# Mamba stages: every queue in the source's order, stores a slot later, less on VectorE, X for one pair

## The chip, the cores and the metric

The kernel runs on one core of one Trainium2 chip, in one launch, in float32. The metric is the device time of the execution in microseconds. A core has five instruction queues that matter here: TensorE (PE, matmuls), VectorE (DVE), ScalarE (ACT), GpSimd (POOL) and SyncE (SP), which issues the transfers (DMAs).

## The reference, cut to what matters

Four layers follow each other on an image batch of 4 x 96 x 64 x 64: a Mamba layer (0), a state-space layer with four scan directions (1), a second Mamba layer like the first (2), and a ConvNeXt block (3). The change is in the code of layers 0 and 2:

```python
def _mamba_block(seq, ...):                      # twice per layer, each time seq = seq + _mamba_block(seq)
    h = layernorm(seq) * ln_g + ln_b
    xs, z = split(h @ in_w)
    xc = silu(causal_conv4(xs) + conv_b)
    dt, Bm, Cm = split(xc @ xproj_w)
    delta = softplus(dt @ dt_w + dt_b)           # (L, 192)
    dA  = exp(delta[..., None] * A)              # (L, 192, 16)
    dBx = delta[..., None] * Bm[:, None] * xc[..., None]
    h_t = dA_t * h_{t-1} + dBx_t                 # the scan along L = 4096
    y = sum_s(h * Cm) + Dp * xc
    return (y * silu(z)) @ out_w
# afterwards
gp  = relu(x.mean((2, 3)) @ gp_w.T + gp_b)       # pooled from the layer's input
out = fus_w @ concat([mamba_out, gp]) + fus_b
out = batchnorm(out) + residual                  # statistics over batch and space
```

## The kernel before

`mamba_fusion` is one Mamba layer. The four images are taken as two pairs; `X` holds the sequence of all four in SBUF. A **step** is one (pair, block, chunk of 512 positions): 2 x 2 x 8 = 32 steps a layer. The 2 x 192 channels of a pair lie on three tiles `j` of 128 partitions.

A step has two halves that run beside each other:

- `mamba_front` is a generator that makes what the next step will scan: layernorm into `h` (matmul with `center`, square, matmul with `mean`, rsqrt on ACT, multiply on DVE L184, scale on POOL L185), convolution and input projection (`pu`, `pz`), the small projection `pd` and `dbl`, then for each `j` the softplus `delta` and `du = delta * xz`. Softplus is: absolute value, exp, log on ACT; on DVE L267, which adds the log to max(x, 0) from PSUM tile `pt`; an identity L268 on ACT that rounds 1+u and writes it back to the PSUM tile; on DVE L270, which makes the rounding error from that tile and `u`; an addition on POOL L271. `delta` and `du` are stored to DRAM (L251, as `dd` and `dg`), since the scan needs each row spread over 16 partitions.
- `Scan.run` scans the step in 24 **groups**: 3 tiles x 4 quarters `q` x 2 halves, of two blocks of 128 x 512 each. A turn of its loop is a **slot**: slot `n` scans group `n`, and does the other stages for groups ahead and behind.

The stages of a group before, with the slot in which each is issued relative to the scan:

| stage | slot | engine and work |
| --- | --- | --- |
| `load` | 4 ahead | SP: `dd` (and for every fourth group `dg`) spread from DRAM into `da` / `du`, L295; six buffers |
| `decay` | 2 ahead | ACT: two exponentials `da`, L107 |
| `spread` | 1 ahead | PE: two matmuls into PSUM `bs` (two banks' pairs), L313; or, for every fourth group, ACT exponentials into `bs` and POOL `du * B`, L308 |
| `scan` | 0 | DVE: `bs * B` L335 (not for the fourth groups), two scans L340; POOL: `hc = hs * C` L342; ACT: last column to `carry` L345 |
| `sums` | 2 after | PE: two matmuls `py` L361, and for each `j` one with `w_dd` L355 |
| `close`, `project`, `fuse` | 3, 4, 5 after the last group of a tile | DVE: `py * silu(z)` L369; PE: `po` L377; DVE: residual add into X L381; for the second block PE `pf` L510, ACT bias L511, DVE batch statistics L512, SP store L513 |

`run` pulls one piece of the generator per slot, by the tuple `PACE`. The order in which each engine gets its instructions is then set by the framework's scheduler, which reorders independent instructions by its own estimate of costs; every engine works through its own list in order.

## Time and profile before

| what | us |
| --- | --- |
| runs | 9810.94, 9851.49, 9849.05 (median 9849.05) |
| profiled execution | 9796.82 (span 9795.1) |
| first Mamba layer, first scan to last | 78 to 3047 |
| second Mamba layer, first scan to last | 6246 to 9197 |
| busy over the span | PE 8426.9, DVE 8142.4, POOL 6879.1, ACT 5527.9 |

The span is the time from the first to the last instruction of the profiled execution. A group line gives the source line, engine, operation, `out<-in` tiles and shape, the count, then the busy time and the mean of one, then the idle time of that engine just before these instructions and what ended it. A wait line gives who waited for whom, the total, how often, and the longest. PEclk in a table of windows is the share of full clock that TensorE was granted.

### The profile page before, as it was taken

How to read it: one execution, taken by the hardware profiler on the slowest of the kernel's cores; microseconds unless marked ns; L12 is line 12 of the kernel's file. 1: busy time of each engine (PE TensorE's matmuls, PEld its weight loads, DVE VectorE, ACT ScalarE, POOL GpSimd, SP SyncE). 2: the span in 40 equal slices, each digit the busy share in tenths (PEclk: the TensorE clock that was granted, in tenths of full speed). 3: DMA queues.
4: the chain of work that ended last, by engine and by line, in shares of the span. 5: the costliest groups of instructions: out<-in, count | busy, mean ns of one | idle time of the engine just before them, and what ended most of it. 6: DMA issues, size and time to landing. Idle time of an engine off the chain costs nothing. (4 is left out here: it accounts for less than half of the span.)

```text
span 9795.1 us, 110014 instructions
## 1 busy us (share of the span) xinstructions
PE 8426.9 (86%) x32750; PEld 3475.8 (35%) x32750; DVE 8142.4 (83%) x11036; ACT 5527.9 (56%) x10516; POOL 6879.1 (70%) x4573
## 2 busy tenths in 40 slices
PE   7888889888887988998888889788888888888678
PEld 1222212222212776776766767212212222222122
DVE  7999999999995666666666667699999999999887
ACT  5666666665663555555555555466666665666345
POOL 6888888888884555555555555588888888888511
PEclk8999999999997999999999999799999999999789
DMA  6677776777774222222222222576777776776653
GB/s 184 201 205 201 205 207 201 203 202 205 206 208 130 73 67 82 83 66 83 82 73 73 86 68 60 157 204 201 207 206 205 211 203 198 210 205 201 166 119 84
DMA packets 808930, 1525.65 MB, mean 156 GB/s; under 512 B 126190, under 2 KB 131722, under 8 KB 804491
## 3 DMA queue, kind: packets, MB, share of 16 engines
q1 hardware_dynamic: 805258, 1513.50, 54.4%
q8 instruction: 260, 4.26, 0.2%
q10 hardware_dynamic: 3072, 5.11, 0.1%
q14 instruction: 340, 2.78, 0.1%
HBM read 1222.99 MB, written 148.50 MB: 140 GB/s over the span
## 5 line engine op out<-in xcount | busy, mean ns | idle before, releaser
L342 POOL TENSOR_TENSOR hc<-hs,bc 128x1024 f32<-128x1024 f32 x1536 | 3610.9, 2358 | 625.5 <-DVE hs L340 545.8
L340 DVE TENSOR_TENSOR_SCAN hs<-da,carry,bs 128x512 f32<-128x512 f32 x2016 | 2466.5, 1264 | 81.0 <-DVE bs L335 2.8
L107 ACT ACTIVATE da<-da,w_a 128x512 f32<-128x512 f32 x2304 | 1616.9, 716 | 1251.7 <-DMA da<-dd 1191.7
L361 PE MATMUL py<-hc,selsum 128*32 128x512 f32 x6144 | 1797.8, 639 | 445.9 <-POOL hc L342 438.9
L313 PE MATMUL bs<-du,seldu 64*128 64x512 f32 x4608 | 1565.3, 675 | 216.0 <-DVE hs L340 203.7
L335 DVE TENSOR_TENSOR bs<-bs,bc 128x1024 f32<-128x1024 f32 x1152 | 1397.7, 1213 | 166.6 <-PE bs L313 163.1
L308 POOL TENSOR_TENSOR du<-du,bc 128x1024 f32<-128x1024 f32 x384 | 905.3, 2358 | 260.3 <-DMA du<-dg 141.0
L361 PEld LDWEIGHTS py<-hc,selsum 128*32 128x32 f32 x6144 | 239.8, 110 | 1791.8 <-POOL hc L342 1097.0
L917 DVE TENSOR_SCALAR seg<-dr,dac 128x128 f32<-128x128 f32 x1536 | 641.2, 451 | 281.9 <-PE y L962 279.5
L313 PEld LDWEIGHTS bs<-du,seldu 64*128 64x128 f32 x4608 | 444.0, 195 | 1205.2 <-DVE hs L340 864.4
L933 POOL TENSOR_TENSOR seg<-seg,cb 128x384 f32<-128x384 f32 x512 | 515.7, 1009 | 475.5 <-DVE cb L932 409.3
L194 PE MATMUL pu<-h,w_conv 96*128 96x512 f32 (+3 forms) x2048 | 833.4, 627 | 8.5 <-ACT rs L107 8.4
L340 DVE TENSOR_TENSOR_SCAN hs<-bs,carry,du 128x512 f32<-128x512 f32 x672 | 823.6, 1260 | 6.2 <-issue 3.2
L868 PE MATMUL front<-pk,sconv 128*128 128x512 f32 x1536 | 755.2, 609 | 27.7 <-ACT z L856 23.8
L972 POOL TENSOR_TENSOR y<-y,xs 128x192 f32<-128x192 f32 x496 | 295.3, 595 | 603.8 <-DVE y L971 587.9
L985 ACT ACTIVATE y<-yz 128x192 f32<-128x192 f32 x512 | 186.1, 363 | 906.2 <-DVE yz L984 905.5
L937 POOL TENSOR_TENSOR xs<-pre,coef 128x576 f32<-128x576 f32 x512 | 598.9, 1175 | 54.0 <-ACT pre L112 24.8
L879 PE MATMUL front<-sconv,pk 128*128 128x192 f32 x3072 | 572.0, 330 | 55.8 <-DVE pre L884 50.5
L345 ACT COPY carry<-hs 128x2 f32<-128x2 f32 x1344 | 250.9, 187 | 566.1 <-DVE hs L340 562.3
L879 PEld LDWEIGHTS front<-sconv,pk 128*128 128x128 f32 x3072 | 496.7, 190 | 87.7 <-DVE pre L884 76.8
L107 ACT ACTIVATE bs<-da,w_a 128x512 f32<-128x512 f32 x768 | 522.0, 680 | 3.1 <-DVE hs L340 1.6
L962 PEld LDWEIGHTS y<-xs,seg 128*128 128x128 f32 x3072 | 437.7, 204 | 142.0 <-issue 80.7
(209 smaller groups left out, 13623.5 us busy)
## 6 DMA issues: line engine op xcount, KB each, us to landing
da<-dd SPq DMA_DIRECT2D x3072, 256.0 KB
du<-dg SPq DMA_DIRECT2D x768, 256.0 KB
dr<-rows SPq DMA_DIRECT2D x256, 384.0 KB
bc<-rows SPq DMA_DIRECT2D x256, 256.0 KB
dd<-delta SPq DMA_DIRECT2D x192, 256.0 KB
dg<-du SPq DMA_DIRECT2D x192, 256.0 KB
pk<-xn SPq DMA_DIRECT2D x128, 384.0 KB
pk<-xn SPq DMA_DIRECT2D x128, 256.0 KB
```

The lines of the kernel that those rows point to most:

```text
L107: self.last = self.scalar.activation(out, in_, func, **kw)
L194: nc.tensor.matmul(pu[r0:r1], lhsT=wt["conv"][:kk, tap, d0:d1], rhs=h[:kk, b, ds(tap, T)], start=(tap == 0), stop=(tap == 3),)
L308: nc.gpsimd.tensor_tensor(g["du"], g["du"], self.b_or_c(g, 0), ALU.mult)
L313: nc.tensor.matmul(g["bs"][:, i], lhsT=self.sel["du"][rows, g["half"], g["q"]], rhs=g["made"]["du"][rows, g["j"]], start=True, stop=True,)
L335: nc.vector.tensor_tensor(dbx, dbx, self.b_or_c(g, 0), ALU.mult)
L340: nc.vector.tensor_tensor_scan(hs[:, i], da[:, i], dbx[:, i], init, ALU.mult, ALU.add)
L342: nc.gpsimd.tensor_tensor(g["hc"], hs, self.b_or_c(g, 1), ALU.mult)
L361: nc.tensor.matmul(py[rows], lhsT=self.sel["sum"][:, g["q"]], rhs=g["hc"][:, i], start=(g["q"] == 0), stop=(g["q"] == NQU - 1),)
L868: nc.tensor.matmul(p, lhsT=self.conv[:, i, DI + q * DST : DI + (q + 1) * DST], rhs=pk[:, i, ds(c * T, T)], start=(i == 0), stop=(i == 2),)
L879: nc.tensor.matmul(p, lhsT=pk[:, i, ds(c * Q, Q)], rhs=self.conv[:, i, :DI], start=(i == 0), stop=(i == 2),)
L917: nc.vector.tensor_scalar(seg[:, h], g["pair"]["dr"][:, c % 2 * NH + h], made["dac"][:, n0 + h : n0 + h + 1], 0.0, ALU.subtract, ALU.min,)
L937: nc.gpsimd.tensor_tensor(xs, x.to_broadcast([P, 3, NH, HD]), coef.to_broadcast([P, 3, NH, HD]), ALU.mult)
```

## The change

1. **Order.** At the end of each turn of `run`, every instruction that the turn issued is chained to the one before it on its engine, SP included, by a dependency that needs no semaphore. Each engine and the transfer queue so get their instructions in the order in which the source issues them.
2. **Lags.** `load` goes from 4 to 5 slots ahead and its buffers from six to eight; `hc` and `carry` move into `after`, issued in the next slot ahead of that slot's scan; `du * B` moves into `product`, two slots ahead; `sums` go from 2 to 3 slots after, `close` from 3 to 4. `hs` and `hc` have four buffers for three. The generator's layernorm is a four-step pipeline with each consumer a piece later, `pd` and `dbl` have pieces of their own, the softplus is split (`softplus` on ACT, `softplus_rest` on DVE a piece later, POOL another piece later), and every store is issued a piece after what it stores. `PACE` and `LEAD` are set anew.
3. **Softplus tile.** 1+u is written to a tile `w` in SBUF instead of back to the PSUM tile.
4. **VectorE.** The residual add becomes a third matmul into `po` with the identity (first block) or the fusion weight (second block) on X; for the second block `w_out` is multiplied by the fusion weight once per layer, so that the fusion needs no matmul of its own. ACT writes the result to X, for the second block with the sum of each row as a second output; a slot later ACT makes the squares' sum around the chunk's mean, in place of DVE's statistics, and a few tiny instructions at the end of the layer join them.
5. **X for one pair.** `X` holds two images. The second pair's chunk is loaded over the first pair's once that has been stored. The pooled sums of the second pair come from eight loads into the `da` buffers.

The core of the diff:

```diff
+IN_ORDER = mybir.DependencyInfo(mybir.DependencyClass.NoSync, mybir.DependencyReason.DATA)
...
-PACE = (1,) * 8 + (2,) + (1,) * 7 + (2,) + (1,) * 7
-LEAD = 4
+PACE = (1,) * 5 + (2, 1, 1, 1) * 2 + (2,) + (1,) * 10
+LEAD = 5
...
-    nc.vector.scalar_tensor_tensor(out, x, 0.0, t, ALU.max, ALU.add)
-    nc.scalar.activation(x, u, AF.Identity, bias=1.0)
-    nc.vector.scalar_tensor_tensor(t, x, 1.0, u, ALU.subtract, ALU.subtract, reverse1=True)
-    nc.gpsimd.tensor_tensor(out, out, t, ALU.add)
+    w = work.tile([P, T], F32, name="wa", bufs=2)
+    nc.scalar.activation(w, u, AF.Identity, bias=1.0)
+    return work.tile([P, T], F32, name="delta", bufs=2), t, u, w, x
+
+def softplus_rest(nc, out, t, u, w, x):
+    nc.vector.scalar_tensor_tensor(out, x, 0.0, t, ALU.max, ALU.add)
+    nc.vector.scalar_tensor_tensor(t, w, 1.0, u, ALU.subtract, ALU.subtract, reverse1=True)
...
+    for n in range(6):
+        for stored in stores:
+            nc.sync.dma_start(*stored)
+        stores = []
+        if 2 <= n < 5:
+            j = n - 2
+            delta, lost = kept.pop(0)[:2]
+            nc.gpsimd.tensor_tensor(delta, delta, lost, ALU.add)
+            nc.gpsimd.tensor_tensor(du[:, j], delta, xz[:, j], ALU.mult)
+            for name, x in (("dd", delta), ("dg", du[:, j])):
+                made[name, j] = dram.tile([P, T], F32, name=f"{name}{j}")
+                stores.append((made[name, j], x))
+        if 1 <= n < 4:
+            softplus_rest(nc, *kept[-1])
...
-        po = self.psum.tile([P, T], F32, tag="po", name="po", bufs=1)[:C]
+        po = self.po = self.psum.tile([P, T], F32, tag="po", name="po", bufs=1)[:C]
+        xs = self.X[:, b, ds(g["c"] * T, T)]
+        nc.tensor.matmul(po, lhsT=wt["of_x"], rhs=xs, start=True, stop=False)
         for n, (j, r0, r1) in enumerate(ROWS[b]):
             nc.tensor.matmul(
-                po, lhsT=wt["out"][r0:r1, j], rhs=xz[r0:r1, j], start=(n == 0), stop=(n == 1)
-            )
-        xs = self.X[:, 2 * g["pair"] + b, ds(g["c"] * T, T)]
-        nc.vector.tensor_tensor(xs, xs, po, ALU.add)
+                po, lhsT=wt["out"][r0:r1, j], rhs=xz[r0:r1, j], start=False, stop=(n == 1)
+            )
+
+    def keep(self, g, b):
+        xs = self.X[:, b, ds(g["c"] * T, T)]
+        if g["sub"] == 0:
+            self.tc.nc.scalar.copy(xs, self.po)
+        else:
+            self.fuse(g, b, xs, self.po)
...
-            if (g := at(3)) and g["last"]:
+            if (g := at(4)) and g["last"]:
                 self.close(g)
             for stage, lag in (
-                (self.load, -4), (self.spread, -1), (self.decay, -2), (self.scan, 0), (self.sums, 2),
+                (self.load, -5), (self.spread, -1), (self.decay, -2), (self.after, 1),
+                (self.product, -2), (self.scan, 0), (self.sums, 3),
             ):
...
-            for lag, what in ((4, self.project), (5, self.fuse)):
+            for lag, what in (
+                (4, self.project), (5, self.keep), (6, self.spread_out), (7, self.reload)
+            ):
...
+            for ins in traced[start:]:
+                if ins.engine not in self.engines:
+                    continue
+                if ins.engine in last:
+                    self.tc.add_manual_dep(ins, last[ins.engine].name, IN_ORDER, reason="order")
+                last[ins.engine] = ins
...
-        nc.vector.bn_stats(stats[:, b * NT + c], xs)
-        nc.sync.dma_start(dst[b, :, ds(c * T, T)], xs)
+    def fuse(g, b, xs, po):
+        n = (2 * g["pair"] + b) * NT + g["c"]
+        nc.scalar.activation(
+            xs, po, AF.Identity, bias=gb[:, n // NT : n // NT + 1], accum_out=sums[:, n : n + 1]
+        )
+
+    def spread_out(g, b):
+        n = (2 * g["pair"] + b) * NT + g["c"]
+        xs = X[:, b, ds(g["c"] * T, T)]
+        nc.scalar.mul(means[:, n : n + 1], sums[:, n : n + 1], -1.0 / T)
+        sq = work.tile([P, T], F32, tag="ua", name="sqs", bufs=2)[:C]
+        nc.scalar.activation(
+            sq, xs, AF.Square, bias=means[:, n : n + 1], accum_out=squares[:, n : n + 1]
+        )
+        nc.sync.dma_start(dst[n // NT, :, ds(g["c"] * T, T)], xs)
```

In the changed kernel L297 and L299 are the two instructions of `softplus_rest`, L369 is the multiply `bs * B`, L374 the scans, L178 the layernorm's multiply and L408 the multiply of `close`.

## The prediction

> **What bounds the kernel now.** I read the page first (busy shares, the 40 slices), then the table of windows, then the groups by line and the waits inside one steady stretch, then single instructions. "DVE" is VectorE, "PE" TensorE, "ACT" ScalarE, "POOL" GpSimd, "SP" the transfer queue. A step is one chunk of one layer for one pair: 24 groups. A slot is one turn of `run`'s loop.
>
> The page's slices show that the edited code runs twice:
>
> ```profile
> DVE  7999999999995666666666667699999999999887
> ```
>
> The stretches at 9 are the two Mamba stages; by the first and last scan they last from 78 to 3047 us and from 6246 to 9197 us, about 5,920 of 9,795 us. The stage between and the tail are not edited. The windows view gives, for 2,400 us inside the first stage and for two slices of it:
>
> ```profile
> core 0: us, PE busy (x) PEld busy (x) DVE busy (x) ACT busy (x) POOL busy (x), PEclk, DMA share, GB/s
> 400.00:2800.00 2400.00, 2098.09 (x6438) 488.05 (x6438) 2246.40 (x2081) 1496.79 (x2677) 2055.26 (x987) 0.96 0.71 204
> 1800.00:1900.00 100.00, 88.74 (x266) 20.59 (x264) 91.15 (x83) 61.24 (x114) 82.82 (x40) 0.91 0.70 201
> 2700.00:2800.00 100.00, 85.49 (x276) 20.10 (x275) 95.37 (x89) 63.04 (x116) 85.92 (x42) 1.00 0.69 204
> ```
>
> DVE is busy 93.6%, with PE (87%) and POOL (86%) close behind. So DVE sets the pace, and what it can gain by waiting less is 6.4%. The two slices show that DVE loses more when the granted clock is 0.91 than at 1.00. The groups of DVE in that stretch (count | busy, mean ns | idle before, releaser):
>
> ```profile
> L340 DVE TENSOR_TENSOR_SCAN hs<-da,carry,bs 128x512 f32<-128x512 f32 x828 | 1013.0, 1264 | 32.9 <-ACT da L107 0.5 <-ACT carry L345 0.5 <-POOL du L308 0.5
> L335 DVE TENSOR_TENSOR bs<-bs,bc 128x1024 f32<-128x1024 f32 x468 | 567.9, 1214 | 69.9 <-PE bs L313 68.2
> L270 DVE SCALAR_TENSOR_TENSOR lg<-pt,ua 128x512 f32<-128x512 f32 x78 | 53.0, 680 | 16.4 <-ACT pt L268 15.9
> L184 DVE TENSOR_TENSOR h<-pc,rs 96x512 f32<-96x512 f32 x52 | 35.1, 676 | 12.5 <-ACT rs L107 12.3
> L381 DVE TENSOR_TENSOR X<-X,po 96x512 f32<-96x512 f32 x52 | 34.7, 668 | 10.9 <-PE bs L313 10.9
> L512 DVE BATCH_NORM_STATS2 stats<-X 96x6 f32<-96x512 f32 x26 | 17.5, 672 | 0.0
> ```
>
> 468 multiplies at 18 a step are 26 steps: 92.3 us a step. Idle per step: 2.69 us before the multiply (PE late), 0.63 before L270, 0.48 before L184, 0.42 before L381, 0.12 before L267 (its row has 3.1), and about 1.5 in the four scan rows, mostly 0.1 us between the multiply and the scan that reads it. Sum 5.9. Most of the 2.69 falls at one place, where the timeline has 2.08 us of `pd` matmuls ahead of `bs` and DVE idle for 1.77 us at 1530.44. Behind it stand these waits of the other engines:
>
> ```profile
> PE py L361 <- POOL hc L342: 167.0, 209, 4.6
> ACT da L107 <- DMA da<-dd: 463.4, 296, 6.3
> SPq L251 <- POOL delta L271: 197.9, 78, 4.6
> ```
>
> PE stops at `py` for POOL with the next `bs` behind it; loads come late for ACT, partly because SP stands at a store. ACT (62%) has room, so its 463 us cost DVE next to nothing.
>
> **What the Trainium skill says.** *PSUM — Partial Sum Buffer*, "Engine vs sequencer instructions": the queues of ScalarE, VectorE and GpSimd are strict FIFO and matmuls complete in program order; so a wait at a queue's head holds all behind it. The waits above agree. *TensorE: Matmul & The Clock Gate*, "The HAM clock gate": TensorE runs at full or half clock. Here the same pair of `py` matmuls took 1.05 us, or 1.92 us at 1555.84. *SBUF — State Buffer*, "Who interferes with whom": a DVE instruction with two SBUF inputs contends with a GpSimd instruction that reads SBUF, and whichever comes second is blocked until the first has ended. Of the DVE instructions before, none in the steady Mamba steps has two SBUF inputs, but in the stage between L984 has, and L971 reads PSUM:
>
> ```profile
> L984 DVE TENSOR_TENSOR yz<-y,z x512: 336/1020/2630, 3158.0 to 6153.5; 128x192 f32<-128x192 f32 x171
> L971 DVE TENSOR_TENSOR y<-y,edac x496: 336/357/363, 3161.4 to 6152.1; 128x192 f32<-128x192 f32 x166
> ```
>
> The timeline of one case (start us, us):
>
> ```profile
> 3335.43 1.32 DVE L984 TENSOR_TENSOR yz<-y,z 128x192 f32<-128x192 f32 x1
> 3335.39 1.15 POOL L937 TENSOR_TENSOR xs<-pre,coef 128x576 f32<-128x576 f32 x1
> ```
>
> Same work (min/median/max ns), but L984 has a median of 1020: it started 0.04 us after a POOL instruction and ended 0.21 us after that one ended. The trace agrees.
>
> **The change, part by part.**
>
> *Work off DVE.* The residual add (L381) becomes a matmul into the same PSUM bank, the batch statistics (L512) sums that ACT gives with its activations. Both Mamba layers together: 128 adds at 0.668 and 64 statistics at 0.672 us, less the 0.04 us by which neighbours overlap (the rows' counts times means give 2,330 us, the union 2,246, over 2,081 instructions): 192 x 0.63 = **-121 us**, all on DVE's path. ACT takes in exchange two copies a step (0.575 us each) in the first block, two pairs of a tiny multiply (0.19) and a square (0.59) in the second, 1.2 to 1.6 us: 57.6 becomes 59 us of 90, covered. PE gets six projection matmuls for five on average, about +1 us a step: covered by its 13% idle. The shorter X frees memory; its eight loads and reductions for the pooled sum stand in place of two long reductions (4.42 us each) before the first scan; two reloads in 8 steps of a layer wait on SP for their store, with the loads three slots ahead.
>
> *Waits.* Sums move from two to three groups behind the scan, stores go a slot behind, `pd` and `dbl` get slots of their own, loads go five ahead with eight buffers instead of four with six. `h` and the softplus tail come a slot after ACT's part. So L184's 0.48 and L381's 0.42 go, L270's 0.63 falls to 0.2, and of L335's 2.69 the bunched part goes. What is late next is PE at half clock: 0.96 means half speed for 8% of the time, 7.4 us a step, 3.7 us of work lost, and the two `bs` banks give only a slot of slack; projections of 3 x 1.06 us ahead of `bs` add to it. I keep 1.4. Sum -2.6 us a step, x 64: **-166 us** (bounds 0 and -270, all but the turn-around).
>
> *The fixed order.* It issues nothing new. What queues behind each waiting instruction: behind SP's stores the loads, with three slots (11 us) until ACT wants them; behind ACT's softplus the exponentials, two slots early; behind PE's `py` the next `bs`. POOL at the softplus slots has two `hc`, a product (2.36 us each) and twice 1.27 us; I walked it and find it under two slots late, which the sums' third slot covers. Cost taken as nothing; the cover failing is the slow case below.
>
> *A lock that comes in.* L270's successor, L299 of the changed kernel, reads `w` and `u`, both now in SBUF; before, `x` stood in PSUM (the identity L268 wrote it there). Three a step. POOL is busy 86%, mostly with instructions of 2.36 us that read SBUF. Undisturbed the price is small: L1262 of the last stage, the same operation from SBUF, has a median of 752 ns against 680. Against a running POOL instruction it is the rest of that one plus about 0.55. Walk: after the scan of group 14 both L297 (0.68, reads PSUM) and POOL's `hc` start; L299 comes 0.6 us later, waits some 1.75 and takes 2.3: +1.6. The second and third meet the product and the 1.27 us instructions somewhere: +0.35 each. I take +2.3 a step, x 64: **+147 us**. Bounds: +0.07 each, 14 us (no gain: L1262 shows none), and +2.2 each, 420 us.
>
> *Ends.* In each Mamba layer's last step DVE waited 5.01 and 2.55 us for `py` (timeline from 2957): -15 for both. The first exponentials now queue behind the next step's layernorm (about 5 us a layer): +10. The closing statistics are a few tiny instructions, within 2 us.
>
> Sum: -121 - 166 + 147 - 5 = **-145 us**. The profiled execution took 9,796.8 us (span 9,795.1), so it would take about 9,652. The runs shown have a median of 9,849, 0.5% above it; the same difference from there is 9,704, rounded to **9,705**.
>
> **Rivals.** (1) *The lock is cheap*, because L299 mostly gets there first: -121 - 250 + 30 = -341, about 9,510 to 9,560. For: an L984 that met no POOL instruction took 336. Against: POOL's 86%. (2) *No change*: L299 meets the full rest of long instructions (+3.4 a step, 218) and PE gives back only 100 us of waits: -121 - 100 + 218 + 10 = +7, 9,856. (3) *Slower, through PE's fixed order*: at both projections three matmuls stand ahead of `bs`, and in half-clock windows everything takes double. From the point where PE is more than one slot (3.7 us) behind the scan, each us is DVE's. Place: groups 3 and 19 of a step. Price: `bs` waits up by 4 us a step instead of down by 1.3: -121 - 98 (the other waits) + 256 + 147 = +184, 10,030. For: PE at 87%, and 1.77 us lost at one bunch before. Against: in the two slots around each projection a group that needs no `bs` follows, and PE's stops for POOL vanish. (4) *The order is not kept*: excluded, the instruction lists of the changed kernel show it.
>
> **How the numbers follow.** Main case 0.56 (9,705, itself 9,610 to 9,800); cheap lock 0.17; no change 0.13; slower 0.14. About 0.5% (49 us) is what a measurement of this kernel can tell from no change. Faster by more: the main case but 0.02, the cheap lock, a little of the third: 0.73; within: 0.13; slower: 0.14. The range, 9,540 to 9,880, takes in the first three but the edge of the cheap lock.
>
> **What would show it.** Right: no DVE add or statistics in the step; L299 at a mean near 1.4 us with a wide spread; the multiply's wait for PE (L369 there) near 1.4 us a step; ACT's wait for `da` far below 463 us; a step near 90 us. Wrong: L299 near 0.75 (then faster), the multiply's wait above 2.7 us a step (then slower), or DVE waiting for ACT at L297.

## The result, and the profile after

The changed kernel takes 9999.26 us (median of 4 runs, 9986.54 to 10019.13) where the kernel before takes 9845.95 in the same comparison (9810.94 to 9851.49). The ratio is 1.0165 [1.0135, 1.0195]: slower, and outside the predicted range of 9,540 to 9,880. The profiled execution has a span of 9989.0 us against 9795.1, at a mean granted clock of 0.912 against 0.941.

By the first and last scan, the Mamba stages now last from 91.5 to 3134.6 us and from 6348.5 to 9391.1 us, 3043 us each, against 2969 and 2951 before. That is 166 of the 194 us by which the span of the profiled execution grew; the other 28 lie ahead of the first scan of the two layers (13 and 14). So the loss lies in the edited stages. The busy shares of DVE over the 40 slices of the page, and the windows view of 2,400 us inside the first stage:

```profile
DVE  7999999999996666766766667699899999899887
```

```profile
core 0: us, PE busy (x) PEld busy (x) DVE busy (x) ACT busy (x) POOL busy (x), PEclk, DMA share, GB/s
400.00:2800.00 2400.00, 2064.67 (x6272) 473.75 (x6270) 2188.55 (x1935) 1435.76 (x2679) 2015.22 (x954) 0.91 0.75 198
```

DVE's busy time in the stretch fell from 2246 to 2189 us, but the stretch also holds fewer steps, as the groups below show. Per step DVE is busy for 2188.55 / 25.06 = 87.3 us, before 2246.40 / 26 = 86.4: the work taken off DVE doesn't show in its busy time, since the three L299 of a step are longer (1.4 us together) and the instructions overlap their neighbours less (1.2 us). The larger part of the loss is waiting, and the groups say for what (count | busy, mean ns | idle before, releaser):

```profile
L374 DVE TENSOR_TENSOR_SCAN hs<-da,carry,bs 128x512 f32<-128x512 f32 x796 | 975.3, 1267 | 46.8 <-DVE bs L369 1.4
L369 DVE TENSOR_TENSOR bs<-bs,bc 128x1024 f32<-128x1024 f32 x451 | 547.1, 1213 | 28.5 <-PE bs L343 28.5
L299 DVE SCALAR_TENSOR_TENSOR lg<-wa,ua 128x512 f32<-128x512 f32 x75 | 85.8, 1145 | 8.5 <-ACT wa L291 0.5 <-ACT da L111 0.5
L408 DVE TENSOR_TENSOR xz<-py,xz 128x512 f32<-128x512 f32 x75 | 51.8, 690 | 38.7 <-PE py L400 38.7
L297 DVE SCALAR_TENSOR_TENSOR delta<-pt,lg 128x512 f32<-128x512 f32 x75 | 50.8, 677 | 20.7 <-ACT lg L111 20.6
L178 DVE TENSOR_TENSOR h<-pc,rs 96x512 f32<-96x512 f32 x50 | 34.2, 684 | 58.4 <-ACT rs L111 58.4
```

Two groups of the kernel before that the prediction doesn't show, for the comparison:

```profile
L267 DVE SCALAR_TENSOR_TENSOR delta<-pt,lg 128x512 f32<-128x512 f32 x78 | 52.7, 676 | 3.1 <-ACT lg L107 2.9
L369 DVE TENSOR_TENSOR xz<-py,xz 128x512 f32<-128x512 f32 x78 | 52.4, 672 | 0.6 <-PE py L361 0.5
```

451 multiplies at 18 a step are 25.06 steps: 95.8 us a step, where it was 92.3. The bunched wait for `bs` did shrink, from 2.69 to 1.14 us a step. In its place stand three others: `h` waits for ACT's `rs` (58.4 / 25.06 = 2.33 us a step, before 0.48), `close` waits for `py` (1.54, before 0.02), `delta` waits for `lg` (0.82, before 0.12). The idle time in the scans' four rows grew too, from 1.54 to 2.27 us a step, for the most part without a releaser; it comes up again at the end of the experiments. DVE's idle time is 8.4 us a step, before 5.9.

The waits of PE in the stretch (who waits for whom: us in total, times, longest us):

```profile
PE bs L343 <- DVE hs L374: 262.6, 102, 6.8
PE pv L184 <- ACT X L425: 36.5, 13, 2.8
PE pv L184 <- ACT X L569: 36.1, 12, 3.0
```

PE's stop at `py` for POOL, 167 us before, is gone, and so is ACT's wait of 463 us for the loads of `da`. New is a wait of `pv`, a matmul of the layer norm, for ACT's copy `X` (`keep`), 72.6 us together. The change puts `pv` into the PSUM tile `po`, of which there is one buffer, so `pv` cannot start until `keep` has read the projection out of it. This line of the diff is not among those shown above:

```diff
-        pv = bank("pv")[:C]
+            pv = psum.tile([P, T], F32, tag="po", name="pv", bufs=1)[:C]
```

The timeline shows this chain once in each step (start us, us, engine, line; in brackets the idle time ahead and its releaser):

```profile
1312.40 2.05 PE L418 MATMUL po<-xz,w_out 128*96 128x512 f32 x4
...
1315.51 0.59 ACT L194 ACTIVATE sq<-pc 96x512 f32<-96x512 f32 x1 [5.58 <-PE pc L190]
1316.01 1.40 ACT L111 ACTIVATE bs<-da,w_a 128x512 f32<-128x512 f32 x2
1317.35 1.32 ACT L111 ACTIVATE da<-da,w_a 128x512 f32<-128x512 f32 x2
...
1318.65 0.68 ACT L569 ACTIVATE X<-po,gb 96x512 f32<-96x512 f32 x1
...
1319.48 1.10 PE L184 MATMUL pv<-sq,mean 96*96 96x512 f32 x2 [3.02 <-ACT X L569]
...
1320.67 0.68 ACT L111 ACTIVATE rs<-pv,eps 96x512 f32<-96x512 f32 x1 [1.25 <-PE pv L184]
1321.39 0.63 ACT L111 ACTIVATE rs<-rs 96x512 f32<-96x512 f32 x1
1321.45 2.08 PE L343 MATMUL bs<-du,seldu 64*128 64x512 f32 x4
...
1322.05 0.69 DVE L178 TENSOR_TENSOR h<-pc,rs 96x512 f32<-96x512 f32 x1 [2.04 <-ACT rs L111]
...
1323.58 1.23 DVE L369 TENSOR_TENSOR bs<-bs,bc 128x1024 f32<-128x1024 f32 x1 [0.84 <-PE bs L343]
```

Read it from the top. The projection `po` is complete at 1314.45. ACT stands idle until 1315.51, for its next instruction is `sq`, which waits for `pc` behind `po` on PE; then it does four exponentials and the carry; `keep` comes only at 1318.65. For 3.02 us PE stands at `pv`. Then `pv`, `rs` and `h` follow without a gap, DVE stands 2.04 us at `h`, and 0.84 us more at the next `bs`, which had to stand behind `pv` and which PE ran at half clock (2.08 us for what takes 1.13 elsewhere; the clock records have half clock there).

### The profile page after: what moved, and what is told of

Same layout as the page of the kernel before. It is cut to its first block, busy times and chain, and to the rows that moved or that the text cites. A ratio compares the mean times of both kernels' runs of the same rounds, so it can differ in the third digit from the quotient of the medians.

```text
span 9989.0 us, 110219 instructions
## 1 busy us (share of the span) xinstructions
PE 8503.0 (85%) x32896; PEld 3493.9 (35%) x32896; DVE 8183.2 (82%) x10870; ACT 5509.4 (55%) x10786; POOL 6954.8 (70%) x4573
## 5 line engine op out<-in xcount | busy, mean ns | idle before, releaser
L381 POOL TENSOR_TENSOR hc<-hs,bc 128x1024 f32<-128x1024 f32 x1536 | 3664.1, 2392 | 663.9 <-DVE hs L374 654.4
L374 DVE TENSOR_TENSOR_SCAN hs<-da,carry,bs 128x512 f32<-128x512 f32 x2016 | 2470.1, 1267 | 119.5 <-DVE bs L369 3.2
L343 PE MATMUL bs<-du,seldu 64*128 64x512 f32 x4608 | 1518.7, 713 | 719.4 <-DVE hs L374 719.2
L400 PE MATMUL py<-hc,selsum 128*32 128x512 f32 x6144 | 1737.8, 650 | 9.2 <-POOL hc L381 9.2
L111 ACT ACTIVATE da<-da,w_a 128x512 f32<-128x512 f32 x2304 | 1520.1, 710 | 0.7
L369 DVE TENSOR_TENSOR bs<-bs,bc 128x1024 f32<-128x1024 f32 x1152 | 1397.3, 1213 | 66.9 <-PE bs L343 66.9
L343 PEld LDWEIGHTS bs<-du,seldu 64*128 64x128 f32 x4608 | 406.6, 202 | 1702.7 <-DVE hs L374 1128.0
L351 POOL TENSOR_TENSOR du<-du,bc 128x1024 f32<-128x1024 f32 x384 | 933.0, 2430 | 0.0
L374 DVE TENSOR_TENSOR_SCAN hs<-bs,carry,du 128x512 f32<-128x512 f32 x672 | 819.1, 1260 | 4.3
L982 PEld LDWEIGHTS front<-sconv,pk 128*128 128x128 f32 x3072 | 497.1, 190 | 88.3 <-DVE pre L987 77.2
L1065 PE MATMUL y<-xs,seg 128*128 128x64 f32 x3072 | 446.7, 282 | 29.4 <-POOL seg L1036 23.9
```

The lines of the kernel that those rows point to most:

```text
L111: self.last = self.scalar.activation(out, in_, func, **kw)
L343: nc.tensor.matmul(g["bs"][:, i], lhsT=self.sel["du"][rows, g["half"], g["q"]], rhs=g["made"]["du"][rows, g["j"]], start=True, stop=True,)
L351: self.tc.nc.gpsimd.tensor_tensor(g["du"], g["du"], self.b_or_c(g, 0), ALU.mult)
L369: nc.vector.tensor_tensor(dbx, dbx, self.b_or_c(g, 0), ALU.mult)
L374: nc.vector.tensor_tensor_scan(hs[:, i], da[:, i], dbx[:, i], init, ALU.mult, ALU.add)
L381: nc.gpsimd.tensor_tensor(g["hc"], hs, self.b_or_c(g, 1), ALU.mult)
```

## The experiments

Ratios are to the kernel before, with 95% intervals. It was measured anew beside each batch of runs: its median was 9845.95 us beside the changed kernel and 9820.91 to 9827.86 beside the other runs. Differences in us below are between medians of different batches, so one of 25 us or less says little by itself. Times in traces are from 400 to 2800 us unless said; step lengths and times at half clock without another count beside them are means over 58 steps, all but the first and the last two of each layer.

### Four runs: the order, the lock, the clock, the layer norm's place

The theories in the expectations are A (PE's standstills bring half clock), L (the lock on L299) and B (the PSUM tile shared by `pv` and the projection).

*no_order* leaves the chain of orders out and keeps the rest of the change:

```diff
-                if ins.engine in last:
-                    self.tc.add_manual_dep(ins, last[ins.engine].name, IN_ORDER, reason="order")
```

> The changed kernel without its chaining of instructions: lags, buffers, split softplus, projection and X stay, and the scheduler may again reorder within each engine. Theory A, the clock: kept strictly in order, TensorE does its part of two slots early and then stands still in one piece (6.5 us at group 16, 3 us at group 20) for the scan; its clock falls to half afterwards (17 us a step against 7 before), and then it is late for VectorE. Without the order other matmuls fill these pieces: half clock back to some 7 to 10 us a step, step from 95.6 to 90-92 us, about 9,700 to 9,800 us. Theory L, the lock: L299 with two SBUF inputs costs VectorE as much without the order (mean above 1.0 us, 1.4 us a step more than its predecessor), so at best 9,850 to 9,900. Theory B, the PSUM bank that the layernorm's pv now shares with the projection: the wait stays, so about 9,950.

Measured: 9686.66 us (9684.16 to 9693.49), 0.9853 [0.9831, 0.9876]. The chain of orders therefore costs 9999 - 9687 = 313 us (3.2% by the ratios), and all the rest of the change together gains 141 against its own measurement of the kernel before. L and B, which expected 9,850 and more, fall as causes of the loss; A's 9,700 is missed by 13. DVE's waits and L299 in its trace:

```profile
DVE bs L369 <- PE bs L343: 64.8, 46, 2.9
DVE xz L408 <- PE py L400: 2.2, 7, 0.4
DVE delta L297 <- ACT lg L111: 0.7, 1, 0.7
...
L299 DVE SCALAR_TENSOR_TENSOR lg<-wa,ua 128x512 f32<-128x512 f32 x81 | 110.6, 1365 | 0.0
```

The wait for `rs` is not among them, those for `py` and `lg` are near nothing; and yet `pv` shares the tile of `po` here too, so the shared tile alone doesn't make the wait. In 476 / 18 = 26.44 steps of 90.8 us DVE idles 4.1 us a step, 4.3 less than in the changed kernel; that is most of the 5.0 us by which the steps differ.

*lock_out* takes L299 out of the lock by reading the PSUM tile instead of the SBUF copy `w`. That tile doesn't hold 1+u in the changed kernel, so what L299 computes here is no longer the rounding error; the work stays the same:

```diff
-    nc.vector.scalar_tensor_tensor(t, w, 1.0, u, ALU.subtract, ALU.subtract, reverse1=True)
+    nc.vector.scalar_tensor_tensor(t, x, 1.0, u, ALU.subtract, ALU.subtract, reverse1=True)
```

> The changed kernel, but L299 takes its first operand from the PSUM tile x instead of the SBUF tile w; what it computes is then not the rounding error of 1+u, the output not the reference's, the instruction and all else the same. Theory L: L299 goes from a mean of 1.145 us to 0.68, three a step, 1.4 us a step for VectorE and the same again in POOL's 2.4 us instructions that it holds up: 64 steps, about 90 us, 9,900 us. Theory A: VectorE gains 1.4 us a step at groups 14 to 16, which shortens TensorE's standstill at group 16 from 6.5 to about 5 us, still long enough for half clock: less than 1.4 us a step gained, 9,930 to 9,990 us, half clock still above 14 us a step.

Measured: 9971.85 us, 1.0143 [1.012, 1.0165]: 27 us less, with an interval that overlaps that of the changed kernel. This is within A's range and 72 us above L's. The lock is there (L299 has a mean of 0.692 us instead of 1.145), and it isn't the loss. Per step DVE is busy about 1.2 us less and idle 0.7 us more: `h` for `rs` went from 58.4 to 73.9 us, the multiply for `bs` from 28.5 to 47.3, while `close` for `py` fell from 38.7 to 20.3.

*warm* keeps PE busy in two places where it stood waiting for the scan, the longest gap among them, with matmuls into `po` that nothing reads. The gap of 3 us at `pv` is not filled:

```diff
+FILL = {12: 1, 16: 5}
...
+            if n % each in FILL and 0 <= n < total:
+                warm = self.psum.tile([P, T], F32, tag="po", name="warm", bufs=1)
+                for _ in range(FILL[n % each]):
+                    self.tc.nc.tensor.matmul(warm, lhsT=self.k.ident, rhs=self.sel["du"][:, 0], ...)
```

> The changed kernel with idle matmuls put into TensorE's queue behind the sums of groups 12 (one) and 16 (five), about 1.05 us each, into the free projection bank, nobody reads them. They are more work, and fill the standstill ahead of the matmul that waits for the scan. Theory A: TensorE no longer stands still at group 16, half clock falls from 17 to 8-10 us a step, VectorE's waits for layernorm, sums and bs shrink, and the kernel gets faster with more work: step 92 to 93.5 us, 9,800 to 9,880 us. Theories L and B: no gain, 9,990 to 10,050 us, since the added matmuls cost or are hidden.

Measured: 10014.39 us, 1.0188 [1.0168, 1.0208]: no gain. The windows view, and two of DVE's groups (L298 and L300 are L297 and L299 here):

```profile
400.00:2800.00 2400.00, 2162.42 (x6563) 525.89 (x6562) 2207.69 (x1933) 1430.59 (x2673) 2010.92 (x952) 0.95 0.75 198
...
L300 DVE SCALAR_TENSOR_TENSOR lg<-wa,ua 128x512 f32<-128x512 f32 x75 | 110.4, 1472 | 8.5 <-ACT da L111 0.5 <-ACT wa L292 0.5
L298 DVE SCALAR_TENSOR_TENSOR delta<-pt,lg 128x512 f32<-128x512 f32 x75 | 50.2, 670 | 0.7 <-DMA dd<-delta 0.3
```

The granted clock is 0.95 in place of 0.91; by the clock records, the time at half clock fell from 17.2 to 10.5 us a step. Three of DVE's waits stayed (`rs` 58.9, `py` 38.2, `bs` 29.2), and the step is 95.8 us. So half clock is not what makes those for `rs` and `py`. The one at `bs` is not settled by this run: behind the unfilled gap at `pv` the `bs` matmuls still take 2.08 us here, 0.95 more than elsewhere, which is as much as DVE waited there (0.84). The wait at L297 did go, 20.7 us to 0.7, but L299 right behind it grew by 24.6 us. In both kernels L299 ends 0.55 us after the POOL instruction that runs when it starts (median 0.546 us in 73 of 75 cases, 0.549 in 74), so starting it sooner only makes it longer: the wait at L297 and the price of L299 are one sum. Theory A falls as the cause of the loss.

*ln_later* puts the layer norm's pieces, and those up to `pd`, one slot later; the softplus keeps its slots:

```diff
-PACE = (1,) * 5 + (2, 1, 1, 1) * 2 + (2,) + (1,) * 10
+PACE = (0,) + (1,) * 4 + (2, 1, 1, 1) * 2 + (2,) + (1,) * 3 + (2,) + (1,) * 6
```

> The changed kernel with the front's first pieces one slot later, so that pv takes the projection's bank a slot after keep has read it; pd and dbl share a slot instead, the rest of the front stays in its slots. Theory B: TensorE's 3.0 us wait of pv for keep goes, and with it VectorE's 2.3 us a step before L178: 64 x 2.3, about 150 us, 9,850 us. Theory A: one of the two standstills goes, half clock falls by some 3 us a step, and 1 to 2 us of the step: 9,870 to 9,940 us; that at group 16 stays. Theory L: nothing but L178's wait moves to another wait, 9,970 to 10,000 us.

Measured: 9902.81 us, 1.0075 [1.0054, 1.0096], 96 us less than the changed kernel. DVE's waits in its trace:

```profile
DVE xz L408 <- PE py L400: 75.1, 63, 3.2
DVE bs L369 <- PE bs L343: 12.4, 25, 0.6
```

The wait for `rs` is gone, as B said, but the one for `py` has doubled, so that B's 9,850 is missed by 53 us. Why `py` is late was not followed further. A's forecast for this run came true in its figures (9,870 to 9,940; half clock 14.1 us a step, 3 less), as in lock_out; it is warm, which cuts the half clock and leaves every order as it is, that speaks against A.

### Four runs: which queue's order is it?

Each leaves one engine (or POOL with SP) to the scheduler and holds the others exactly as in the changed kernel, by the list of engines to be chained; *free_pe* for example:

```diff
-        self.engines = [e.engine for e in (nc.tensor, nc.vector, nc.scalar, nc.gpsimd, nc.sync)]
+        self.engines = [e.engine for e in (nc.vector, nc.scalar, nc.gpsimd, nc.sync)]
```

> The changed kernel with the order written out for four engines only: PE is left to the scheduler, and the order of DVE, ACT, POOL and SP stays as it is. Theory P (the loss sits in PE's queue: PE reaches the projections' pc and pv and the read-out py late because it may not pass a bs that waits for a scan, so rs and xz come late to DVE): 9,700 to 9,760, DVE's waits for rs, py and lg together fall from 118 us in 400:2800 to under 40. Theory S (ACT's queue: carry and the exps stand ahead of what DVE waits for): 9,960 to 10,010, the waits as they are. Theory M (no single queue; several are stiff at once): 9,850 to 9,930.

> The changed kernel with ACT alone left to the scheduler. Theory P: 9,960 to 10,010, no change beyond the spread. Theory S: 9,700 to 9,780, DVE's waits for rs and lg go. Theory M: 9,850 to 9,930.

> The changed kernel with DVE alone left to the scheduler. Theories P and S: 9,960 to 10,010, since what DVE waits for is late whatever DVE does ahead of it, and the wait only moves to another row. Theory D (DVE's own fixed order makes the wait: other work lay ready that it may not take): 9,700 to 9,800, DVE's idle time falls from 8.3 us per step to about 3.

> The changed kernel with POOL and SP left to the scheduler, PE, DVE and ACT held. Theories P, S and D: 9,960 to 10,010. Theory Q (the stores and loads held on SP, or hc held on POOL, make the inputs late): 9,700 to 9,800, with PE's waits for DVE in 400:2800 well below 262 us.

| run | left to the scheduler | us | ratio | `h` waits for `rs`, us |
| --- | --- | --- | --- | --- |
| changed kernel | none | 9999.26 | 1.0165 [1.0135, 1.0195] | 58.4 |
| free_pe | PE | 10037.23 | 1.0218 [1.0201, 1.0235] | 102.9 |
| free_act | ACT | 9990.89 | 1.0174 [1.0159, 1.019] | 61.1 |
| free_dve | DVE | 10104.92 | 1.0292 [1.0276, 1.0308] | 66.4 |
| free_queues | POOL, SP | 10186.26 | 1.0373 [1.0358, 1.0389] | 71.5 |

P, S, D, Q and M, each of which foresaw a gain from one of these runs, all fall: freeing a single queue doesn't take the loss away, and three of the four are worse. For free_act the reason can be read in the timeline, at the same place of a step:

```profile
1312.77 0.67 ACT L569 ACTIVATE X<-po,gb 96x512 f32<-96x512 f32 x1
...
1314.29 1.10 PE L184 MATMUL pv<-sq,mean 96*96 96x512 f32 x2 [0.41 <-ACT sq L194]
...
1317.79 0.72 ACT L111 ACTIVATE da<-da,w_a 128x512 f32<-128x512 f32 x1 [2.47 <-DMA da<-dd]
1318.41 0.67 ACT L111 ACTIVATE rs<-pv,eps 96x512 f32<-96x512 f32 x1
...
1320.12 0.69 DVE L178 TENSOR_TENSOR h<-pc,rs 96x512 f32<-96x512 f32 x1 [2.67 <-ACT rs L111]
```

ACT now takes `keep` ahead of `sq`, and PE's wait for `keep` is gone. But the scheduler has put an exponential ahead of `rs`, its load arrives late, and DVE waits at `h` as long as before. The free engine has been ordered by estimated times that the held ones don't keep. In free_pe it is PE that stands at `py` for POOL's `hc`, 196.2 us, a wait that PE doesn't have in the changed kernel. In free_dve DVE idles no more than there (8.2 us a step against 8.4); it is busier, by 2.1 us a step, and the line that grew is L299:

```profile
L299 DVE SCALAR_TENSOR_TENSOR lg<-wa,ua 128x512 f32<-128x512 f32 x75 | 164.0, 2186 | 0.0
```

In free_queues L299 has a mean of 1.933 us. So these two runs are slower mostly through the lock, not through the chain seen in the timeline, though the wait for `rs` stays in both.

### Four runs: one slot of one copy

*keep_early* issues ACT's `keep` in the slot of the projection instead of the next one. The order stays chained on all five:

```diff
-                (4, self.project), (5, self.keep), (6, self.spread_out), (7, self.reload)
+                (4, self.project), (4, self.keep), (6, self.spread_out), (7, self.reload)
```

> The changed kernel, all five orders held, with the projection's copy keep one slot earlier: ACT takes it in the slot of project, ahead of the layer norm's sq. Theory K (the fixed order ties close on DVE, po on PE, keep and sq on ACT, pv on PE, rs on ACT and h on DVE into one chain with no slack, which crosses three engines so that freeing any one doesn't help; in the trace keep starts at 81.0 us of the step though po is ready at 75.2, since it stands behind a sq that waits 5.6 us): PE's wait of pv for keep (72.6 us in 400:2800) and DVE's wait of h for rs (58.4) go, and with them the wait for bs that follows (about 20): some 2.5 to 3 us of each of 62 steps, 9,800 to 9,860. Theory R (the ring moves: PE then runs late at py of group 3, as with the later layer norm): the h wait goes and the wait for py grows from 38.7 to over 70, 9,890 to 9,950. No effect: 9,960 to 10,020.

Measured: 9804.07 us (9780.96 to 9817.4), 0.9979 [0.9969, 0.999]: 195 us less than the changed kernel, as theory K put it, and level with the kernel before. The wait for `py` didn't grow (33.5 us), so R falls. The timeline at the same place:

```profile
1275.10 2.05 PE L418 MATMUL po<-xz,w_out 128*96 128x512 f32 x4
...
1277.19 0.68 ACT L569 ACTIVATE X<-po,gb 96x512 f32<-96x512 f32 x1 [4.63 <-PE po L418]
...
1278.22 0.59 ACT L194 ACTIVATE sq<-pc 96x512 f32<-96x512 f32 x1 [0.17 <-PE pc L190]
...
1279.09 1.10 PE L184 MATMUL pv<-sq,mean 96*96 96x512 f32 x2
...
1281.36 0.68 ACT L111 ACTIVATE rs<-pv,eps 96x512 f32<-96x512 f32 x1
...
1282.73 0.69 DVE L178 TENSOR_TENSOR h<-pc,rs 96x512 f32<-96x512 f32 x1
```

ACT's idle time now lies ahead of `keep`, for `po`, instead of ahead of `sq`, for `pc`; all that was changed is that `keep` stands ahead of `sq`, the four exponentials and the carry instead of behind them: `pv` starts 1.94 us after the end of `po` instead of 5.03, PE doesn't stop, and `h` has no wait. And DVE's groups:

```profile
L369 DVE TENSOR_TENSOR bs<-bs,bc 128x1024 f32<-128x1024 f32 x468 | 567.4, 1212 | 0.1
...
L299 DVE SCALAR_TENSOR_TENSOR lg<-wa,ua 128x512 f32<-128x512 f32 x78 | 91.5, 1173 | 8.8 <-ACT da L111 0.5 <-ACT wa L291 0.5
L408 DVE TENSOR_TENSOR xz<-py,xz 128x512 f32<-128x512 f32 x78 | 53.8, 690 | 33.5 <-PE py L400 33.5
...
L178 DVE TENSOR_TENSOR h<-pc,rs 96x512 f32<-96x512 f32 x52 | 35.1, 675 | 1.0 <-ACT rs L111 0.6
```

The wait for `rs` fell from 58.4 to 0.6 us, and the multiply's for `bs` from 28.5 to nothing: 2.33 + 1.14 = 3.5 us a step, and the step went from 95.7 to 92.3. Time at half clock fell with them to 13.5 us a step, and is still nearly twice the 7.2 of the kernel before, which is no slower. That `pv` shares the tile of `po` is as much a part of this chain as the late copy; no run gives `pv` a tile of its own again, so how much that would bring is not known.

*free_pe_act* and *hold_pe_act* are complements: the first chains DVE, POOL and SP, the second PE and ACT.

```diff
-        self.engines = [e.engine for e in (nc.tensor, nc.vector, nc.scalar, nc.gpsimd, nc.sync)]
+        self.engines = [e.engine for e in (nc.vector, nc.gpsimd, nc.sync)]      # free_pe_act
+        self.engines = [e.engine for e in (nc.tensor, nc.scalar)]               # hold_pe_act
```

> The changed kernel with PE and ACT both left to the scheduler; DVE, POOL and SP held. Theory K: keep, sq, pc and pv lie on these two engines, so with both free the wait for rs falls below 20 us in 400:2800 and the time to 9,720 to 9,850. Theory D2 (DVE's held order alone is enough for the loss, whatever the others may do): 9,960 to 10,050, h still waits for rs.

> The changed kernel with only PE and ACT held; DVE, POOL and SP left to the scheduler. Theory K: the chain stays on the two held engines, 9,960 to 10,150, PE still waits for keep by about 70 us in 400:2800. Theory D2: 9,720 to 9,850.

Measured: free_pe_act 9872.89 us, 1.0053 [1.0037, 1.0068], its wait for `rs` 47.7 us; hold_pe_act 10051.53, 1.0228 [1.0213, 1.0243], with PE's wait of `pv` for `keep` at 36.5 + 36.1 us, the same as in the changed kernel. So the order of PE and ACT alone is enough for the whole loss, and freeing these two together gives back 126 us where freeing either gave back 8 or lost 38. K had expected more of free_pe_act: it misses both K's upper end, by 23 us, and K's figure for `rs`. D2 is out.

*no_order_lock* is no_order with the edit of lock_out.

> The changed kernel without the chain of orders, and L299 reading x in PSUM in place of the copy w in SBUF, so that it does not share POOL's lock. From the parts: 9,687 without the chain; in its trace L299 takes 1.365 us against 0.68 for the PSUM form before, 0.68 x 3 x 64 = 131 us if all of it counts (9,560), and 27 us if it counts as in the held order (9,660). Theory L (the lock is on DVE's path, which is the bound without the chain): 9,560 to 9,620. Theory F (POOL or ACT gives it back): 9,640 to 9,690.

Measured: 9743.07 us, 0.9919 [0.9899, 0.9938], 56 us slower than no_order; both theories missed. L299 came down to a mean of 0.669 us from 1.365, as it should; but without the chain the edit also moves the scheduler's order on the engines, and the multiply's wait for `bs` went from 64.8 to 127.0 us. As a test of the lock this run is not clean.

### Five runs: what is left

Between keep_early and no_order 117 us remain.

*keep_start* is keep_early with the chain beginning at slot 1, so that each layer's start is free:

```diff
-                if ins.engine in last:
+                if ins.engine in last and n > 0:
```

> keep_early with the order written out only from slot 1 on (if n > 0), so that the start of each layer is left to the scheduler. Theory E (part of what is left, 9,804 against 9,687 without the chain, is the start: the first scan comes at 92.2 us instead of 79.3 in the first layer, and as late in the second): 9,770 to 9,785. Otherwise (the steps behind the start take it back): 9,795 to 9,815.

Measured: 9802.78 us, 0.998 [0.9973, 0.9988]. Theory E falls. The first scan does come at 79.7 us instead of 92.2, but the first step then takes 102.5 us instead of 88.4.

*keep_lock* is keep_early with the edit of lock_out, so it doesn't compute the rounding error either.

> keep_early with L299 reading x in PSUM in place of w in SBUF. In keep_early's trace L299 has a mean of 1.173 us against 0.68 for the form before: 0.49 x 3 x 64 = 95 us on DVE. Theory L2 (with the chain's wait gone, DVE's busy time is the bound, and the lock is worth more than the 27 us that it was worth in the changed kernel): 9,710 to 9,760. Theory F2 (POOL or a PSUM bank held longer gives part of it back): 9,765 to 9,800.

Measured: 9769.91 us, 0.995 [0.9933, 0.9967], 34 us less, the upper of the two cases (F2). DVE's work shrank by 0.48 us three times a step, and two thirds of it came back as a wait of `close` for `py`, from 33.5 to 58.4 us.

*keep_free_pe* is keep_early with PE left to the scheduler, by the list of engines as in free_pe.

> keep_early with PE left to the scheduler, the other four held. Left on DVE in keep_early's 400:2800 are the waits for py (33.5 us) and for lg (20.5), both behind PE's fixed order: 54 us in 26 steps, 129 us of the run. Theory P2 (PE's held order is the rest): 9,680 to 9,760. Theory K2 (as before, the scheduler's own PE order puts a new wait in its place, py for POOL's hc as in free_pe): 9,800 to 9,880.

Measured: 9926.55 us, 1.0098 [1.007, 1.0125], slower than keep_early by 122 us, more than K2 said. P2 falls: PE's held order is not what is left. The waits for `bs` (43.4 us) and `rs` (42.5) come back when PE alone is ordered by estimates, and PE stands 189.0 us at `py` for POOL's `hc`, as K2 said.

*pad1* and *pad3* add a `memset` of 128x512 on DVE behind one or all three closes of a step, into a tile that nothing reads:

```diff
         self.tc.nc.vector.tensor_tensor(xz[:, j], g["made"]["py"], xz[:, 3 + j], ALU.mult)
+        if j == 0:                                    # pad1; pad3 without this line
+            self.tc.nc.vector.memset(self.pad, 0.0)
```

> keep_early with one more instruction on DVE per step, a memset of 128x512 into a tile that nothing reads, behind close of j = 0; it is the work added, and the result stays the same. Its price is taken as that of the other DVE passes over 128x512, about 0.68 us. In the changed kernel 43 of 58 step lengths lie within 0.15 us of 95.57, which is 28 clock windows of 3.413 us; in keep_early 30 of 58 lie as near to 92.16, 27 windows. Theory W (with all orders held a step settles on a whole number of windows; a small saving or loss is swallowed, a larger one costs or brings a whole window): 9,795 to 9,820, the steps stay at 92.2. Theory N (no such rest: what DVE gets more to do, it takes longer): 9,835 to 9,860.

> keep_early with that memset behind each of the three closes of a step, some 2.0 us per step. Theory W: the steps sit either still near 92.2 or mostly near 95.6, 9,795 to 9,820 or 9,970 to 10,030, and few between. Theory N: 9,915 to 9,950, the step 94.3 on the average and spread about it.

Measured: pad1 9927.17 us, 1.0106 [1.0084, 1.0129]; pad3 9938.86, 1.0115 [1.0092, 1.0137]. Neither theory holds for pad1. W is out: of the 58 steps counted in each of the two kernels none lies within 0.15 us of a whole number of windows. N has pad3's figure, but is out for pad1 by some 70 us. In pad1's groups

```profile
L299 DVE SCALAR_TENSOR_TENSOR lg<-wa,ua 128x512 f32<-128x512 f32 x78 | 118.5, 1520 | 8.1
...
L410 DVE MEMSET pad<- 128x512 f32 x26 | 12.6, 485 | 1.4
```

the new instruction takes 0.485 us a step, but the step grew by 1.85 (from 92.34 to 94.19). L299 has a mean of 1.520 instead of 1.173 us: three times 0.35 is 1.04, and DVE's idle time grew by 0.5. L299 was not edited; it meets POOL's instructions at a worse moment. In pad3, with two more of them, L299 has a mean of 1.394, and only 12 us are added, so that N's figure there is a coincidence of two errors.

So what was found by experiment is the larger part, 195 of 313 us: one copy that stood a slot too late. The other 117 are not settled by a run. The start is not among them, PE's order alone is not, and the lock is not, for no_order pays more for it (L299 at 1.365 us against 1.173). The traces show where they lie, though. In keep_early the scan follows its multiply at once; in no_order another instruction often stands between (first keep_early, then no_order):

```profile
1276.35 1.21 DVE L369 TENSOR_TENSOR bs<-bs,bc 128x1024 f32<-128x1024 f32 x1
1277.69 2.45 DVE L374 TENSOR_TENSOR_SCAN hs<-da,carry,bs 128x512 f32<-128x512 f32 x2
...
1301.82 1.21 DVE L369 TENSOR_TENSOR bs<-bs,bc 128x1024 f32<-128x1024 f32 x1
1302.93 0.68 DVE L408 TENSOR_TENSOR xz<-py,xz 128x512 f32<-128x512 f32 x1
1303.53 2.44 DVE L374 TENSOR_TENSOR_SCAN hs<-da,carry,bs 128x512 f32<-128x512 f32 x2
```

The scan that reads the multiply's result starts 0.13 us after its end. With `close` between them, each starts 0.08 to 0.10 us before the one ahead has ended. The held order has 17.9 such pairs a step without anything between, no_order 12.9; and L299 always follows L297 at once (0.10 us), in no_order never. All gaps and overlaps between neighbours on DVE, those of 0.15 us and more left out, add up to -1.8 us a step in keep_early and -3.8 in no_order: 2.0 us a step, 125 us in 64 steps. The longer gaps are 0.3 us a step more in keep_early, and L299 is cheaper there by 0.6 in three, so that 1.7 us is the sum, near the 1.75 us by which the steps of that stretch differ. This is worked out from the traces and not tested: no run changes the neighbours alone, and where DVE was left to the scheduler (free_dve, hold_pe_act) they are as close as in no_order (-3.6 and -3.4), but L299 rose to 2.186 and 1.812 us.

The fastest kernel with all orders held that computes the same as the changed one is keep_early, at 9,804 us. The fastest of all is no_order, at 9,687 us, 1.5% under the kernel before.

## Why the prediction was wrong, point by point

**What bounds the kernel** held: DVE stays the bound. Of the 3.5 us by which a step grew, 2.5 are idle time on DVE and 0.9 busy time.

**Work off DVE (-121)** held. The groups of L381 and L512 are gone, and DVE runs 1935 / 25.06 = 77.2 instructions a step, not 2081 / 26 = 80.0: three fewer, as counted. In DVE's busy time the gain doesn't show: it was outweighed by the lock and by the lost overlap of neighbours, on which the prediction counted as if it stayed.

**Waits (-2.6 us a step)** is the term that failed, in sign: they rose by 2.5. Its first half was right (the multiply's wait fell to 1.14; 1.4 was said). What it said would go did not: L178's wait was to vanish since "`h` and the softplus tail come a slot after ACT's part", and it went from 0.48 to 2.33; `close`, not named at all, got 1.54; the tail was to wait 0.2 and waits 0.82 at L297 and 0.34 at L299; the scans' rows, taken as fixed, went from 1.54 to 2.27. The difference of 5.1 us a step, over 64 steps, is 326 us, and 9,705 + 326 = 10,031 lies near what was measured; some of that is chance, since a layer's first step didn't lengthen (91.8 and 91.3 us, before 100.2 and 96.7).

**The fixed order ("Cost taken as nothing")** is the step behind it. It lists what queues behind SP's stores, ACT's softplus, PE's `py` and POOL, and leaves out two things that the diff shows; keep_early, which mends the first, took 195 us away. First, `sq` on ACT waits for `pc` and has `keep` queued behind it. Second, `pv` now shares the one buffer of `po` with the projection, so that `keep`, which had seemed a harmless copy off the path, releases the layer norm. The prediction itself had cited the Trainium skill (*PSUM — Partial Sum Buffer*, "Engine vs sequencer instructions") for ScalarE's queue being strictly first in, first out, and had concluded that a wait at its head holds all behind it. The 5.58 us at `sq` in the timeline, with `keep` behind, agree; the conclusion was not carried to this queue. A slot between issue and use counts as cover only if the producer runs in its own slot. The 117 us that are left of the 313 also belong to this step, but through DVE's neighbours, as far as the traces show, and untested.

**The lock (+2.3 us a step)** looks over-sized: L299 has a mean of 1.145 us against 0.680, 0.465 x 3 = 1.4 a step. But by place its three means are 1.47, 0.98 and 0.99 us, and the first is shorter because L297 ahead of it comes 0.82 us late. In warm, where L297 is on time, they are 2.39, 0.97 and 1.05: 2.4 us a step, with +1.7 for the first, close to the walk's +1.6, +0.35 and +0.35. Its "plus about 0.55" is right too. Without the chain the lock costs 2.05 (1.365). What the prediction did not say: taking it away is worth only 27 or 34 us in a held order, since most of what DVE saves it waits.

**Ends (-5)**: the first scans come 13 and 14 us later, which was not foreseen; the first steps are 8 and 5 us shorter in return. keep_start shows that an earlier first scan brings nothing.

**The sum.** Without the order, -145 was said, and no_order gave -141. That is partly chance: its idle time fell by 1.8 us a step, not 2.6, and its lock cost 2.05, not 2.3.

**Rivals.** The third had the side and, with 10,030, nearly the time, for another reason. It placed the loss at groups 3 and 19, in the wait for `bs`, through PE's order. By group, DVE's idle time is 1.0 us at 3 and 0.55 at 19, but 2.7 at 22, of which 2.0 are the wait for `rs`; the wait for `bs` fell; and PE left to the scheduler made it slower. "Against: PE's stops for POOL vanish" was true and did not matter. Half clock did rise, from 7.2 to 17.2 us a step, and warm shows that removing two thirds of the rise brings no time back.

**What would show it.** "Wrong: DVE waiting for ACT at L297" came true, as did L299's wide spread and the end of ACT's wait for `da`; the step near 90 us is there in no_order only. The multiply's wait, given as the sign of the slower case, stayed below its 2.7 us.

## What to carry to other kernels

When a queue's order is fixed by hand, follow each chain that crosses engines from buffer to buffer, and for every instruction that may wait write down what stands behind it on the same engine, the small copies that free a PSUM buffer above all: here one such copy, one slot too late, cost 195 us. Freeing one engine from a fixed order is no test of that engine's order, since it will be ordered by times that the others don't keep; moving one instruction is. Shortening or moving an instruction that shares a lock is no clean test either, since a wait ahead of it and its own length can trade places. A gain in work and a loss in order that come in one change should be measured apart: here they were about -141 and +313 us.

## What the runs showed of the hardware that was not expected

- L299, with both inputs in SBUF, ends at a fixed distance behind POOL. In the changed kernel 73 of its 75 executions start while a POOL instruction runs that has over 0.1 us left, and all of these end 0.543 to 0.552 us after that instruction; in no_order it is 80 of 81, 0.546 to 0.568 us. With one input in PSUM (lock_out) it takes 0.691 to 0.693 us whenever it starts.
- So the price of L299 depends on when it meets POOL. Its mean went from 1.112 us (free_act) to 2.186 (free_dve) over kernels in which neither it nor POOL's instructions had been edited, and was 0.67 to 0.69 where one input came from PSUM. A 0.485 us instruction elsewhere in the step moved it by 0.35.
- On DVE a scan that reads the result of the multiply just ahead starts 0.13 us after its end (median, changed kernel), while an instruction that doesn't need the one ahead starts about 0.08 us before that one has ended.
- In six kernels the step lengths crowd at a multiple of the clock window, which is 3.413 us by the records: within 0.15 us of 28 windows (95.57) lie 43 of 58 steps of the changed kernel, 41 of warm's and 32 of lock_out's; of 27 (92.16) 30 of keep_early's and 35 of keep_start's; of 29 (98.98) 33 of free_queues'. A held order repeats its step, so these are few independent cases and not many, and chance is not excluded; ln_later (3), keep_lock (10), pad1 and pad3 (none) hold all orders and don't do it. Why it happens is open.
